# Two state-space mixers: a chunk of 128 tokens is worked as two blocks of 64 on the halves of the partitions

## The chip, the cores and the metric

The kernel runs on one core of one Trainium2 chip, in one launch. The metric is the device time of that launch in microseconds (us). An engine's name in the profile: PE is the tensor engine (matmuls), PEld its weight loads, DVE the vector engine, ACT the scalar engine, POOL the GpSimd engine, SP the engine that issues most DMAs. SBUF is the on-chip memory of 128 partitions, PSUM the matmuls' output memory, eight banks of 512 fp32 values on each of 128 partitions.

## The reference, cut to what matters

Four layers follow each other on x of 4 sequences x 1024 tokens x 512 channels, fp32, each as `x = x + layer(layernorm(x))`: mixer A, a feed-forward layer, mixer B, the same feed-forward layer again. The two mixers are state-space layers. After an input projection, a causal convolution of four taps and silu, both compute, for every head with channels p,

```
state[t] = state[t-1] * exp(a[t]) + (dt[t] * x[t]) outer B[t]      a[t] = -exp(A_log) * softplus(...)
y[t]     = C[t] . state[t] + D * x[t]
```

Mixer A has 16 heads of 64 channels and a state of 64 values for each channel, mixer B 64 heads of 16 channels and a state of 128. Reference A writes the recurrence in chunks of 64 tokens: inside a chunk `M = (C B^T) * exp(segment sums of a)` and `Y_diag = M x`, between chunks a carried state, `Y_off = exp(cumsum a) * (C . state)`. Reference B is a scan over tokens with the same result. The kernel may choose its own chunks.

## The kernel before, in words

Tokens go in chunks of P = 128, two chunks (GC) to a group of 256 tokens; a sequence has 8 chunks, four sequences 32 chunks, 16 groups. A mixer runs over its groups. For each group `front` projects (`convolve`, `gate`: fp32 matmuls of 128x128 weights on 256 or 259 columns, L347), and for each chunk `chunk` does the recurrence. The engines PE, DVE, ACT and POOL run exactly in the order in which the program writes their instructions. `chunk` is a generator: at each `yield us` it lets the driving loop at the end of `mixer` put in pieces of the next group's `front` (a gate counts 1.75, a convolution 1.9) until the yielded amount is used up. `small` and `later_on` hold short steps (transposes, `project_dt`, sums) that are slipped in behind single large matmuls.

What `chunk` does, with the names and lines that matter later:

- `decays(t)`: for 16 heads, the decay matrices exp(cs[l] - cs[s]) for all 128 x 128 pairs of tokens. Four PSUM banks `seg`, four heads in each: first a mask for the pairs in the wrong order inside each half (L797, bf16, two matmuls of 64x64 with 256 columns per bank, -32768 where masked), then the difference of sums as a product of 21 rows with 512 columns (L807, fp16, the four row groups of the array; row 20 masks the upper right quarter), then exp on ACT into `L` (L814, 128x512 at a time).
- `weigh`: DVE multiplies `L` by `Gm` = C B^T with the triangle (L821, 128x1024 at a time).
- `inner`: the weighted sums over source tokens, fp32 matmuls of 128 rows (tokens) x 32 channels in mixer B (four tiles beside each other in the array's columns), 128x64 in A (two tiles), 128 columns each (L837), into the one PSUM bank `py`. Mixer B has four sets of 16 heads (`decays(0)` to `decays(3)`), A one.
- `from_state`: C . state (L855) and its scaling on DVE into `yo` (L859); `open_y` transposes `yo` into `py` (L868); `close_y` adds `py` to h (L886), squares on ACT, multiplies by the gate on POOL (L890).
- the state: POOL makes `hdr` (L927) and scales the old state (L936); `to_state` multiplies (L906) and DVE adds (L917).
- `tail` is the output projection of the chunk before (L669) and its norm; it stands behind the first `decays` of a chunk. `lay_sums`, at the chunk's end, issues on SP the DMAs that bring the cumulated sums of the next chunk from DRAM into the rows `past` and `upto`.

Every fp32 matmul of the program is two MATMUL records in the profile, one for each of two passes. PSUM: seven banks `mm`, handed round, and one for `py`. In mixer B `left`, the last 12 of the 32 tiles, also get the last steps of the first feed-forward layer inside `norm`, which adds DVE work there.

Of the kernel before, what the change touches and what calls it, by code (L numbers as in the profile page):

```python
# [9 lines left out]
BF16 = mybir.dt.bfloat16  # L10
# [5 lines left out]
P = 128  # L16
GC = 2
GT = GC * P
D = 512
# [7 lines left out]

A_MIN = -200.0  # L30
# [42 lines left out]
def hybrid_kernel(  # L73
# [85 lines left out]
    )  # L159

    later = const.tile([P, P], BF16, tag="later", name="later")
    nc.vector.tensor_scalar(later, le, 1.0, -MASKED, ALU.subtract, ALU.mult)
    ident16 = const.tile([P, P], BF16, tag="ident16", name="ident16")
    nc.vector.tensor_copy(ident16, ident)
# [18 lines left out]
    flags = const.tile([P, 2 * HB + 3], F32, tag="flags", name="flags")  # L183
    heads4, first2, row20 = flags[:, :HB], flags[:, 2 * HB : 2 * HB + 1], flags[:, 2 * HB + 2 :]
    pasts = [const.tile([P, SETS, P], F16, tag=f"past{i}", name=f"past_{i}") for i in range(2)]
    sums = [const.tile([P, SETS, HB, P], F16, tag=f"upto{i}", name=f"upto_{i}") for i in range(2)]

    def lay_constants():
        eye = ident.rearrange("p (r w) -> p r w", w=32)
        for i, at in enumerate(  # L190
            [slice(2 + h + 10 * lo, 7 + h + 10 * lo, 4) for lo in (0, 1) for h in range(HB)]
            + [slice(10 * lo, 10 * lo + 2) for lo in (0, 1)]
            + [slice(20, 21)]
        ):
            nc.vector.tensor_reduce(flags[:, i : i + 1], eye[:, :, at], mybir.AxisListType.XY, ALU.add)
        nc.vector.scalar_tensor_tensor(
            heads4, flags[:, HB : 2 * HB], 1.0 / LO_SCALE, heads4, ALU.mult, ALU.add
        )
        nc.vector.scalar_tensor_tensor(
            first2, flags[:, 2 * HB + 1 : 2 * HB + 2], 1.0 / LO_SCALE, first2, ALU.mult, ALU.add  # L200
        )
        for past in pasts:
            nc.vector.tensor_scalar_mul(
                past.rearrange("p t s -> p (t s)"), first2.to_broadcast([P, SETS * P]), -1.0
            )
            nc.vector.tensor_scalar(past[:, :, 64:], past[:, :, 64:], row20, None, ALU.add)

    def lay_flags(sets):
        for upto in sums:
            for t in sets:  # L210
                nc.vector.tensor_copy(upto[:, t], heads4.unsqueeze(2).to_broadcast([P, HB, P]))
                nc.vector.scalar_tensor_tensor(
                    upto[:, t, :, :64],
                    row20.unsqueeze(1).to_broadcast([P, HB, 64]),
                    MASKED,
                    upto[:, t, :, :64],
                    ALU.mult,
                    ALU.add,
                )
# [27 lines left out]
    def mixer(m, in_w, conv_w, conv_b, dt_bias, A_log, Dv, norm_w, out_w, src, dst, first, stats, last_steps={}):  # L247
# [9 lines left out]
        LB = 4  # L257
        SH = P // N
        SW = E // SH
        NE = 2 * NH + NH // SH  # L260
# [5 lines left out]
        with stack:  # L266
            wk = stack.enter_context(tc.tile_pool(name=f"wk_{m.name}", bufs=1, reuse_waits="tile"))
            sm = stack.enter_context(tc.tile_pool(name=f"sm_{m.name}", bufs=2, reuse_waits="tile"))
            p_mm = stack.enter_context(tc.tile_pool(name=f"mm_{m.name}", bufs=7, space=PSUM))
# [119 lines left out]
            def norm(f, prev):  # L389
# [35 lines left out]
                xnT = f.xnT = wk.tile([P, KD, HIST + GT], F32, tag="xnT", name=f"xnT_{tag}", bufs=3)  # L425
# [17 lines left out]
            def front(f, behind):  # L443
# [34 lines left out]
                def silu(j):  # L478
# [13 lines left out]
                    if j % 2 == 0:  # L492
                        f.hs.append(wk.tile([P, 2, GT], F32, tag="h", name=f"h_{tag}_{j}", bufs=8))
                    nc.vector.scalar_tensor_tensor(f.hs[-1][:, j % 2, :], th, 1.0, u, ALU.add, ALU.mult)
# [24 lines left out]
                def gate(n):  # L519
# [14 lines left out]
                    if q == 1:  # L534
                        tz = wk.tile([P, 512], F32, tag="t2k", name=f"tz_{tag}_{rr}", bufs=4)
# [8 lines left out]
                def softplus():  # L544
# [6 lines left out]
                    exu = wk.tile([P, 512], F32, tag="t2k", name=f"exu_{tag}", bufs=4)  # L551
# [21 lines left out]
                    parts = wk.tile([P, 512], F32, tag="t2k", name=f"parts_{tag}", bufs=4)  # L573
# [19 lines left out]
                    ncs = wk.tile([P, 512], F32, tag="t2k", name=f"ncs_{tag}", bufs=4)  # L593
# [63 lines left out]
            state = {"S": None, "tail": iter(())}  # L657

            def tail(f, c, sqs):
# [7 lines left out]
                for e in range(KE):  # L667
                    on = dict(start=(e == 0), stop=(e == KE - 1))
                    nc.tensor.matmul(pout, f.hs[e // 2][:, e % 2, cols], w_out[:, e, :], **on)  # L669
                po = wk.tile([P, D], F32, tag="t2k", name=f"out_{tag}", bufs=4)  # L670
# [34 lines left out]
            def prologue(f, c):  # L705
# [7 lines left out]
                def turn(half, q):  # L713
# [3 lines left out]
                    nc.tensor.transpose(tp[:, q * P : (q + 1) * P], f.hs[half * 2 + q // 2][:, q % 2, cols], ident)  # L717
# [13 lines left out]
                def skip(half):  # L731

                    for e in range(4 * half, 4 * half + 4):
                        h = f.hs[e // 2][:, e % 2, cols]
                        nc.scalar.activation(h, h, AF.Identity, scale=Dc[:, e : e + 1])

                def sums_of(q):
# [5 lines left out]
                    elif q < 3:  # L743
                        nc.tensor.matmul(
                            misc[:, P + (q - 1) * NH : P + q * NH], (le, gt)[q - 1], f.a[:, c, :], start=True, stop=True
                        )
                    elif q == 3:
                        for i in range(SH):
                            nc.tensor.matmul(
                                misc[i * N : i * N + N, P + 2 * NH : P + NE],  # L750
                                ones[:, :N],
                                f.a[:, c, i * NH // SH : (i + 1) * NH // SH],
                                start=True,
                                stop=True,
                                skip_group_check=True,
                            )
                    else:
                        nc.tensor.transpose(misc[:, P + NE : P + NE + N], f.Bc[:, cols], ident[:N, :N])
                        Gm = wk.tile([P, P], F32, tag="Gm", name=f"Gm_{tag}", bufs=2)
                        nc.vector.tensor_mul(Gm, misc[:, :P], le)  # L760
# [10 lines left out]
            def chunk(f, c, following):  # L771
# [13 lines left out]
                el, er, et = ea[:, :NH], ea[:, NH : 2 * NH], ea[:, 2 * NH :]  # L785
# [4 lines left out]
                def decays(t):  # L790

                    sg = [mm(f"seg_{tag}_{t}_{r}").rearrange("p (h l) -> p h l", h=HB) for r in range(4)]

                    for r in range(4):
                        for q in range(2):
                            at = slice(64 * q, 64 * q + 64)
                            nc.tensor.matmul(  # L797
                                sg[r][at, :, at],
                                ident16[at, at],
                                later[at, at].unsqueeze(1).to_broadcast([64, HB, 64]),  # L800
# [4 lines left out]
                    for r in range(4):  # L805
                        rows = slice(32 * r, 32 * r + 21)
                        nc.tensor.matmul(  # L807
                            sg[r], past[rows, t, :], upto[rows, t], start=False, stop=True, skip_group_check=True
                        )
                    Ls = []  # L810
                    for r0 in (0, 2):
                        L = wk.tile([P, 2, HB, P], F32, tag="L", name=f"L_{tag}_{t}_{r0}", bufs=LB)
# [5 lines left out]
                def weigh(Ls):  # L818
                    for L in Ls:
                        Lr = L.rearrange("p r h l -> p (r h) l")  # L820
                        nc.vector.tensor_mul(Lr, Lr, Gm.unsqueeze(1).to_broadcast([P, 2 * HB, P]))  # L821
# [4 lines left out]
                def inner(t, Ls, half, py, started):  # L826

                    for n in range(2 * HB):
                        if CG == 4:

                            u, cg = divmod(n, CG)
                            e, r, hq = 2 * t + half, cg // 2, cg % 2 * 2 + u
                        else:
                            r, hq = divmod(n, HB)
                            e, cg, u = 4 * half + 2 * r + hq // 2, hq % 2, 0
                        h = e * HT + cg * HC + u
                        nc.tensor.matmul(  # L837
                            py[cg * CT : (cg + 1) * CT, e % 4, :],
                            hdt[:, h // HC, u : u + HC, :],
                            Ls[half][:, r, hq, :],  # L840
                            start=not started[cg],
                            stop=False,
                            skip_group_check=True,
                        )
                        started[cg] = True
# [3 lines left out]
                def from_state():  # L849

                    pos = []
                    for half in range(2):
                        rows, hsl = state_at(half)
                        po = mm(f"po_{tag}_{half}")
                        nc.tensor.matmul(po, Cc[rows, cols], state["S"][rows, hsl], start=True, stop=True)  # L855
                        pos.append(po)
                    for half, po in enumerate(pos):
                        tmp = wk.tile([P, 512], F32, tag="yo", name=f"yo_{tag}_{half}", bufs=2)
                        nc.vector.tensor_mul(  # L859
                            heads_of(tmp), heads_of(po), over_head(el[:, half * HALF : (half + 1) * HALF], P, HALF)  # L860
# [3 lines left out]
                def open_y(half):  # L864
                    py = p_y.tile([P, 4, P], F32, tag="y", name=f"py_{tag}_{half}")
                    if not begin:
                        for q in range(4):
                            nc.tensor.matmul(  # L868
                                py[:, q, :],
                                tmps[half][:, q * P : (q + 1) * P],  # L870
                                ident,
                                start=(q == 0),
                                stop=False,
                                is_transpose=True,
                                skip_group_check=True,
                            )
                    return py, [not begin] * CG
# [3 lines left out]
                def close_y(half, py):  # L881

                    sq = wk.tile([P, 4, P], F32, tag="sq", name=f"sq_{tag}_{half}", bufs=2)
# [596 lines left out]
```

## Time and profile before

| | |
|---|---|
| time, median of 3 runs (lowest, highest) | 3009.26 us (3006.67, 3010.05) |
| span of the profiled execution, first to last instruction | 3010.1 us, 46168 instructions |
| mixer A, 75 to 1050 us of the span | PE busy 958.53 of 975 us, DVE 683.30, ACT 386.56, POOL 211.16 |
| mixer B, 1360 to 2765 us | PE busy 1271.17 of 1405 us, DVE 1051.88, ACT 627.50, POOL 298.90 |
| matmul records | 17156 |

The page gives no time of the profiled execution other than its span; the three runs lie within 3.4 us of it. Busy time of PE is the union of records whose ends are modelled: a record lasts some 0.16 us longer than it holds the array, so in dense work start-to-start distances tell the cost and durations don't. In the timeline a row is a run of like instructions: start, length to the last end, count; in brackets the idle time before it and what ended it. "DVE L_b L821" means that the wait ended with the instruction of line 821 that writes a tile named L of mixer B.

### The profile page before, as it was taken

The page shows a single profiled execution, that of the slowest core. Times are in us where ns is not written, and L with a number is a line of the kernel's source. Part 1 is how long each engine was busy: PE and PEld are TensorE (multiplying, and loading weights), DVE is VectorE, ACT ScalarE, POOL GpSimd, SP SyncE. Part 2 cuts the span into 40 slices and gives each one's busy share as a digit, 9 for nine tenths or more (in the row PEclk, how much of TensorE's full clock was granted, in tenths as well). Part 3 has the DMA queues.
Part 4 walks back from the last instruction along what each step waited for, and adds up shares of the span by engine and source line. Part 5 has one row for each costly group of instructions (what it writes and reads, how often), then busy time and mean ns, then how long its engine had stood idle before and what let it go on. Part 6 is the DMA issues. An engine that isn't in the chain of part 4 may idle for free. (4 is left out here: it accounts for less than half of the span.)

```text
span 3010.1 us, 46168 instructions
## 1 busy us (share of the span) xinstructions
PE 2761.4 (92%) x17156; PEld 1785.4 (59%) x17156; DVE 2085.2 (69%) x4417; ACT 1259.9 (42%) x2874; POOL 721.1 (24%) x839
## 2 busy tenths in 40 slices
PE   7999999999999989989999999998989889898986
PEld 6666666666666643456666656666656566564332
DVE  5677677666777652677777677767788777876268
ACT  3334434443344332454444444444444444444244
POOL 1122122222222220531211111212232222212057
PEclk9999999999999989999999999999999999999998
DMA  3000000000000025520000000000000000002423
GB/s 119 10 24 17 17 17 24 18 17 17 21 20 17 10 94 188 177 76 15 11 19 21 20 14 20 15 13 24 20 24 24 18 24 20 13 12 83 160 95 105
DMA packets 92960, 124.27 MB, mean 41 GB/s; under 512 B 38728, under 2 KB 42328, under 8 KB 92736
## 3 DMA queue, kind: packets, MB, share of 16 engines
q1 hardware_dynamic: 80960, 98.23, 10.2%
q10 hardware_dynamic: 9792, 16.82, 1.5%
q0 software_dynamic: 1984, 6.26, 0.6%
q8 instruction: 137, 2.24, 0.3%
q14 instruction: 87, 0.71, 0.1%
HBM read 84.54 MB, written 36.72 MB: 40 GB/s over the span
## 5 line engine op out<-in xcount | busy, mean ns | idle before, releaser
L347 PE MATMUL pc_b<-xnT_b,w_in_b 128*128 128x259 f32 x1280 | 358.0, 408 | 17.8 <-DVE S_b L917 16.7
L821 DVE TENSOR_TENSOR L_b<-L_b,Gm_b 128x1024 f32<-128x1024 f32 x256 | 308.9, 1249 | 2.8 <-ACT L_b L814 2.8
L347 PE MATMUL pz_a<-xnT_a,w_in_a 128*128 128x256 f32 x1024 | 303.5, 410 | 3.0 <-ACT Bt_a L764 2.3
L347 PE MATMUL pc_a<-xnT_a,w_in_a 128*128 128x259 f32 x1152 | 302.5, 397 | 0.0
L347 PE MATMUL pz_b<-xnT_b,w_in_b 128*128 128x256 f32 x1024 | 298.7, 402 | 3.2 <-ACT xnT_b L436 3.2
L814 ACT ACTIVATE L_b<-seg_b 128x512 f32<-128x512 f32 x512 | 263.4, 600 | 78.2 <-PE seg_b L807 78.1
L474 DVE SCALAR_TENSOR_TENSOR u_b<-pc_b,cw_b,u_b 128x256 f32<-128x256 f32 x480 | 231.7, 483 | 84.5 <-ACT u_b L470 73.0
L347 PEld LDWEIGHTS pc_b<-xnT_b,w_in_b 128*128 128x128 f32 x1280 | 229.4, 199 | 84.5 <-DVE S_b L917 20.3
L837 PE MATMUL py_b<-L_b,hdt_b 128*32 128x128 f32 x4096 | 162.8, 294 | 109.3 <-DVE L_b L821 108.3
L474 DVE SCALAR_TENSOR_TENSOR u_a<-pc_a,cw_a,u_a 128x256 f32<-128x256 f32 x432 | 208.5, 483 | 78.5 <-ACT u_a L470 68.2
L1218 PE MATMUL g_ps<-gw,xnT_f 128*128 128x512 f32 x512 | 251.7, 629 | 11.3 <-DMA gw<-in_L_ffn_gate_w 4.6
L347 PEld LDWEIGHTS pc_a<-xnT_a,w_in_a 128*128 128x128 f32 x1152 | 202.8, 192 | 59.5 <-DVE rs_a L684 11.4
L669 PE MATMUL pout_a<-w_out_a,h_a 128*128 128x512 f32 x512 | 230.3, 603 | 0.0
L669 PE MATMUL pout_b<-w_out_b,h_b 128*128 128x512 f32 x512 | 228.3, 599 | 0.0
L890 POOL TENSOR_TENSOR h_b<-h_b,z_b 128x256 f32<-128x256 f32 x128 | 91.3, 734 | 508.7 <-ACT sq_b L889 508.7
L347 PEld LDWEIGHTS pz_b<-xnT_b,w_in_b 128*128 128x128 f32 x1024 | 175.7, 196 | 48.8 <-issue 28.0
L837 PEld LDWEIGHTS py_b<-L_b,hdt_b 128*32 128x32 f32 x4096 | 110.3, 115 | 158.6 <-DVE L_b L821 63.8
L347 PEld LDWEIGHTS pz_a<-xnT_a,w_in_a 128*128 128x128 f32 x1024 | 169.1, 194 | 48.8 <-ACT out_a L689 19.7
L1218 PEld LDWEIGHTS g_ps<-gw,xnT_f 128*128 128x128 f32 x512 | 95.1, 199 | 126.9 <-issue 117.0
L669 PEld LDWEIGHTS pout_a<-w_out_a,h_a 128*128 128x128 f32 x512 | 95.5, 192 | 116.0 <-issue 111.9
L669 PEld LDWEIGHTS pout_b<-w_out_b,h_b 128*128 128x128 f32 x512 | 94.6, 190 | 114.6 <-issue 111.3
L889 ACT ACTIVATE sq_b<-h_b 128x256 f32<-128x256 f32 x128 | 47.9, 417 | 260.5 <-DVE h_b L886 260.5
(321 smaller groups left out, 4903.9 us busy)
## 6 DMA issues: line engine op xcount, KB each, us to landing
d<-in_L_ffn_d_w SPq DMA_DIRECT2D x4, 2048.0 KB
x_f<-xa SPq DMA_DIRECT2D x32, 256.0 KB
xb<-x_b ACTq DMA_DIRECT2D x32, 256.0 KB
x_f<-xb SPq DMA_DIRECT2D x32, 256.0 KB
x_a<-in_L_attn_a_x SPq DMA_DIRECT2D x30, 256.0 KB
xa<-x_a ACTq DMA_DIRECT2D x30, 256.0 KB
out<-x_f SPq DMA_DIRECT2D x22, 256.0 KB
xf<-x_f SPq DMA_DIRECT2D x20, 256.0 KB
```

Of the source, the lines that this page charges most:

```text
L347: nc.tensor.matmul(*args, **kw)
L474: nc.vector.scalar_tensor_tensor(u, ps[:, k : k + GT], cw[:, j, k : k + 1], u, ALU.mult, ALU.add)
L669: nc.tensor.matmul(pout, f.hs[e // 2][:, e % 2, cols], w_out[:, e, :], **on)
L814: nc.scalar.activation(L[:, r], sg[r0 + r], AF.Exp)
L821: nc.vector.tensor_mul(Lr, Lr, Gm.unsqueeze(1).to_broadcast([P, 2 * HB, P]))
L837: nc.tensor.matmul(py[cg * CT : (cg + 1) * CT, e % 4, :], hdt[:, h // HC, u : u + HC, :], Ls[half][:, r, hq, :], start=not started[cg], st ...
L889: nc.scalar.activation(sr, yh, AF.Square)
L890: nc.gpsimd.tensor_mul(yh, yh, zs[half * 2 + r][:, :, cols])
L1218: nc.tensor.matmul(ps, xnT[:, k, :], gw[:, k, :], start=(k == 0), stop=(k == KD - 1 and not bias_on_pe))
```

## The change

A chunk is still 128 tokens, but is treated as two blocks of 64 (BL, NQ = 2), one on partitions 0 to 63, one on 64 to 127.

- Decays are made inside the blocks only: `L` has 64 columns per head in place of 128. One call of `decays` fills its four banks with two sets of 16 heads in mixer B (NS = 2; in A NS = 1 and half a bank each), so B has two calls in place of four and half as many exps and weighs.
- The masks become products too: 24 constant rows (`mask_past`, `mask_upto`, fp16), one 24x64 weight tile and 512 columns (256 in A) per bank and block, and 7 further constant rows inside `past` and `upto` (27 rows in place of 21). The weight tiles are 32 rows x 64 columns of the array, eight of them.
- `inner` becomes matmuls of 64 rows (tokens) x 32 channels (64 in A) with 64 columns, one for each block, into two PSUM banks `py[0]`, `py[1]`.
- Between the blocks the state is carried: POOL scales the old state S0 into `S1`, `to_state` adds the first block's product to it, POOL scales that into `S2`, and the second block's product is added to it behind `weigh(L0)`. `from_state` uses S0 for the first block and S1 for the second, so the first chunk of a sequence now has a `from_state` (second block) and the last a `to_state` (first block). `hdr` is kept in the buffer of S2. The state's products move to the front of the chunk, before `weigh(L0)` and `from_state`.
- Banks: `mm` 6 in place of 7, `py` 2 in place of 1. `xnT` 2 buffers in place of 3; the tiles `h` hold four channel tiles in place of two; `yo` moves into the pool `t2k` (5 buffers in place of 4). The amounts yielded are others. A is cut at -88 in place of -200.

The core of the diff:

```diff
                 def decays(sets):
+                    for r in range(4):
+                        rows = slice(32 * r, 32 * r + 24)
+                        for b, at in enumerate(blocks):
+                            nc.tensor.matmul(sg[r][at].rearrange("p t h l -> p (t h) l"), mask_past[rows, b, :],
+                                mask_upto[rows].unsqueeze(1).to_broadcast([24, NS * HB, BL]), start=True, stop=False, ...)
-                            nc.tensor.matmul(sg[r][at, :, at], ident16[at, at], later[at, at]...to_broadcast([64, HB, 64]), ...)
-                        rows = slice(32 * r, 32 * r + 21)
-                        nc.tensor.matmul(sg[r], past[rows, t, :], upto[rows, t], start=False, stop=True, ...)
+                    for n, t in enumerate(sets):
+                        for r in range(4):
+                            rows = slice(32 * r, 32 * r + 27)
+                            for at in blocks:
+                                nc.tensor.matmul(sg[r][at, n], past[rows, t, at], upto[rows, t, :, at], ...)
-                        L = wk.tile([P, 2, HB, P], F32, tag="L", ..., bufs=LB)
+                        L = wk.tile([P, 2, NS, HB, BL], F32, tag="L", ..., bufs=LB)
                             nc.scalar.activation(L[:, r], sg[r0 + r], AF.Exp)
...
                 def inner(t, Ls, half, py, started):
+                    for n in range(2 * HB // CG):
+                        for b, at in enumerate(blocks):
+                            for cg in range(CG):
+                                nc.tensor.matmul(py[b][cg * CT : (cg + 1) * CT, e % 4, :],
+                                    hdt[at, h // HC, u : u + HC, :], Ls[half][at, r, t % NS, hq, :], ...)
-                        nc.tensor.matmul(py[cg * CT : (cg + 1) * CT, e % 4, :], hdt[:, h // HC, u : u + HC, :], Ls[half][:, r, hq, :], ...)
...
                 def to_state(part):
+                    pst = [mm(f"pst_{tag}_{part}_{b}") for b in range(1 if end else NQ)]
+                            nc.tensor.matmul(pst[b][rows], Bt[blocks[b]], hdr[blocks[b], half * 512 : half * 512 + 512], ...)
+                        nc.vector.tensor_add(S1[:, hsl], S1[:, hsl], pst[0])          # a copy at the sequence's start
+                    if not end:
+                        nc.gpsimd.tensor_mul(heads_of(S2[:, hsl]), heads_of(S1[:, hsl]), over_head(over, P, 512 // HD))
+                    return hsl, pst[-1]
...
-                L0 = decays(0)
+                L0 = decays(range(NS))
                 next(last, None)
-                if not begin:
-                    from_state()
+                nc.gpsimd.tensor_mul(hdr...)
+                if not begin:
+                    nc.gpsimd.tensor_mul(heads_of(S1), heads_of(S0[:, :SW]), over_head(et[0], P, NH // SH))
+                yield 2.2
+                carried = [to_state(part) for part in range(2 // SH)]
+                weigh(L0)
+                if not end:
+                    for hsl, pst in carried:
+                        nc.vector.tensor_add(S2[:, hsl], S2[:, hsl], pst)
+                next(last, None)
+                yield 2.8
+                from_state()
                 if CG == 4:
+                    L1 = decays(range(NS, TS))
+                    yield 2.8
+                    py, on = open_y(0)
+                    for t in range(NS):
+                        for half in range(2):
+                            inner(t, L0, half, py, on)
+                    weigh(L1)
+                    yield 2.4
+                    close_y(0, py)
+                    yield 2.4
+                    py, on = open_y(1)
+                    for t in range(NS, TS):
+                        for half in range(2):
+                            inner(t, L1, half, py, on)
+                    yield 2.0
+                    close_y(1, py)
```

`open_y` now has for each half and each of the four channel tiles two transposes of 64 rows x 128, one per block; `close_y` adds the two banks, 256 values each; the sums of `a` over a block (`misc`) take two matmuls in place of one. New constants are laid once at the start of the kernel, on POOL and DVE.

## The prediction

> **What bounds the kernel now.** I read the page's busy shares first, then the busy time by stage, then PE's waits in each mixer, then the timeline of a chunk.
>
> ```profile
> PE 2761.4 (92%) x17156; PEld 1785.4 (59%) x17156; DVE 2085.2 (69%) x4417; ACT 1259.9 (42%) x2874; POOL 721.1 (24%) x839
> ```
>
> ```profile
> 75.00:1050.00 975.00, 958.53 (x5177) 647.88 (x5178) 683.30 (x1604) 386.56 (x969) 211.16 (x277) 1.00 0.06 17
> ...
> 1360.00:2765.00 1405.00, 1271.17 (x9731) 862.10 (x9729) 1051.88 (x2010) 627.50 (x1456) 298.90 (x316) 0.96 0.07 21
> ```
>
> The rows by stage give length, then PE, PEld, DVE, ACT, POOL, granted clock. Mixer A (first) is PE: 16 us idle in 975, clock 1.00. Mixer B is PE with holes: 134 us idle in 1405, clock 0.96. These two stages hold all that changes. PE's waits in B:
>
> ```profile
> PE py_b L837 <- DVE L_b L821: 108.3, 86, 5.3
> PE pc_b L347 <- DVE S_b L917: 16.7, 12, 2.2
> ```
>
> So `inner` of B waits for DVE's weighing, up to 5.3 us at a time. The pieces of a chunk that the change rewrites, in B and then in A:
>
> ```profile
> 1964.74 0.60 PE L868 MATMUL py_b<-ident,yo_b 128*128 128x128 f32 x4
> 1965.27 1.08 PE L837 MATMUL py_b<-L_b,hdt_b 128*32 128x128 f32 x32
> 1966.28 2.00 PE L347 MATMUL pz_b<-xnT_b,w_in_b 128*128 128x256 f32 x8
> ...
> 1973.51 1.04 PE L717 MATMUL tph_b<-ident,h_b 128*128 128x128 f32 x8
> ...
> 1982.81 1.88 PE L855 MATMUL po_b<-S_b,Cc_b 128*128 128x512 f32 x4
> 1984.53 0.60 PE L347 MATMUL pz_b<-xnT_b,w_in_b 128*128 128x256 f32 x2
> ...
> 1989.81 0.62 PE L797 MATMUL seg_b<-later,ident 64*64 64x256 bf16 x8
> 1990.36 0.39 PE L807 MATMUL seg_b<-upto,past 21*128 21x512 f16 x4
> 1990.69 0.61 PE L678 MATMUL ssq_b<-ones,sq_b 128*128 128x1 f32 x4
> ...
> 2000.61 1.98 PE L906 MATMUL pst_b<-hdr_b,Bt_b 128*128 128x512 f32 x4
> 2002.42 0.60 PE L347 MATMUL pz_b<-xnT_b,w_in_b 128*128 128x256 f32 x2
> ```
>
> ```profile
> 510.76 1.13 PE L855 MATMUL po_a<-S_a,Cc_a 64*128 64x512 f32 x4
> 511.82 0.70 PE L347 MATMUL pz_a<-xnT_a,w_in_a 128*128 128x256 f32 x2
> ...
> 522.69 1.09 PE L837 MATMUL py_a<-L_a,hdt_a 128*64 128x128 f32 x16
> 523.71 3.77 PE L347 MATMUL pc_a<-xnT_a,w_in_a 128*128 128x259 f32 x16
> ```
>
> From start to next start: a `decays` costs 1990.69 - 1989.81 = 0.88 us, a burst of 32 `inner` records in B 1.01, one of 16 in A 1.02, `po_b` 1.72, `pst_b` 1.81, `po_a` 1.06. Eight full transposes last 1.04 with the last record 0.27 long: 0.77 / 7 = 0.11 us per 128 fp32 columns. Thus B's 32 records are eight rounds of four tiles at 0.11 (0.88) and 0.13 for entering and leaving the tiled mode. Tiles in different columns run beside each other; so do different rows: the four products of L807 (385 ns each by its group) are over in 0.39, and two row tiles at a time do `po_a`'s four 512-column records in 1.06, where `po_b` in full width takes 1.72.
>
> **The change part by part, on PE.** I take a round of 64 columns as half of 0.11, 0.055.
> 1. `decays`. Before 128 calls in B, 32 in A: 113 and 28 us. L807's 512-column stream with leaving the mode is 0.33, so 0.22 of it stream. After, in B: masks one round of eight tiles with 512 columns (0.22), products two rounds with 256 (0.22), mode 0.11: 0.55, 64 calls, 35 us; in A half the columns, 0.33 x 32 = 11. Gain 78 + 17. If only four tiles go at once: 1.0 x 64 and 0.55 x 32, gain 49 + 10.
> 2. `inner`. Before 128 bursts in B x 1.01 = 129, 64 in A x 1.02 = 65: 194 us for 5120 records. After 10240 records with half the columns: in B 64 bursts of 128, eight tiles at once, 16 rounds x 0.055 + 0.15 = 1.03, 66 us; in A 64 bursts of 32, four at once, 8 x 0.055 + 0.15 = 0.59, 38 us. Gain 90. Nothing in the trace shows rows and columns of fp32 tiles together. The other end is half as many tiles at once, at the old 0.11 per round: 64 x 3.65 + 64 x 1.9 = 355, a loss of 160. I take the gain, since rows alone and columns alone both run beside each other; with half the tiles and 0.055 it is 1.9 and 1.03 per burst, 188, a gain of 6.
> 3. `open_y`: eight transposes of 64 rows in four pairs, each loading 128 columns of weights as before: same stream, one more mode change per half (0.1 x 128 halves), +13; ends -26 (a pair at 0.055) and +53 (no pairs).
> 4. State products: same streams, in pairs. B newly enters tiled modes, 0.1 x 3 x 32 = +10. First and last chunks of the four sequences gain work: B (1.72 + 0.3 + 1.81) x 4 = 15, A (1.06 + 0.3 + 1.0) x 4 = 9. Together +34; ends +20 and +60.
> 5. One more sum matmul per block in `misc`: +7. The new constants at the start stand on DVE and POOL before the first convolution: some 16 short operations of 0.2 to 0.5 us, +5 (0 to 10).
> PE's work: -78 - 17 - 90 + 13 + 34 + 12 = -126 us.
>
> One rule speaks against part 2. The Trainium skill, "TensorE: Matmul & The Clock Gate", "Back-to-back issue gap", puts a floor of about 25 ns under each matmul of up to 64 columns. By it 10240 records would need 256 us against 194, and the total below would come out near 2959. The row of L807 disagrees for different tiles: its four records of 385 ns are over in 0.39 us, so that their starts lie within some 10 ns.
>
> **The waits.** DVE in B loses half of L821:
>
> ```profile
> L821 DVE TENSOR_TENSOR L_b<-L_b,Gm_b 128x1024 f32<-128x1024 f32 x256 | 308.9, 1249 | 2.8 <-ACT L_b L814 2.8
> ...
> L814 ACT ACTIVATE L_b<-seg_b 128x512 f32<-128x512 f32 x512 | 263.4, 600 | 78.2 <-PE seg_b L807 78.1
> ```
>
> that is -154 us on DVE and -132 on ACT, both beside PE. It gains 120 - 56 = 64 state additions of 0.68 (+44) and contention: L980 needs 425 ns at best and up to 2042 with a POOL operation running, and now POOL's S2 product runs beside `weigh(L0)`; 1 us per chunk, +32 (0 to 60). DVE comes to about 975 us. POOL gains one state product per chunk (about 2 us), off the path: it has the 7 us of `tail` for `hdr` and S1. SP's DMAs keep their place.
>
> The 108 us go: L0 is weighed two pieces and a `from_state` before `inner` reads it. Late next is the scaled state `yo`. Between `pst` and `yo` DVE must do S1 (1.4), two weighs with contention (3.5), S2 (1.4), the tail's row of short operations (2.6), two convolutions with silu (3.7), `yo` (1.4): 14 us. (The tail's row waits for POOL's rsqrt, which now stands behind S2 in POOL's queue; S2's 2 us are over while DVE weighs.) PE in the meantime has `pst` 1.8, two to three pieces with their small matmuls at about 2.2, `po` 1.7, `decays` 0.55: 8.5 to 10.7. It is the same queue that holds the banks: four of six `mm` banks stay with `pst`, two of them until S2. I price the new waits at 2.6 us in each of B's 32 chunks, 83 us against the 134 idle now: -51; ends -134 (nothing waits) and +25 (5 us per chunk). The clock of 0.96 costs 4% of 1405 = 56 us; shorter waits should bring half back, -28; ends 0 and -56. In A one bank less and one more addition: 0 to +30, I take +2.
> Sum: 3010.1 - 126 - 51 - 28 + 2 = 2807 us; the profiled execution stands 0.8 us above the median of the runs, which I leave.
>
> **Rivals.**
> - Narrow tiles give nothing (`inner` 188 us in place of 104): 2807 + 84 = 2891. For it: no row shows eight fp32 tiles. Against: both halves of the claim are shown alone.
> - The waits only move (idle time and clock stay): 2807 + 79 = 2886, with 5 us per chunk 2965. For it: DVE at 975 of some 1220 us is busier than now, 80% against 75%. Against: the longest waits, 5.3 us, have their cause removed.
> - Slower, by one mechanism: the pace of records in `inner`. Today's 5120 records cost 38 ns each with their loads. If the 10240 need 35 ns (rounds not wider than today and not shorter), the loss of 160 replaces the gain of 90: 3057. It decides from 30 ns per record, (104 + 203) / 10240.
> - All waits vanish and the clock returns to 1.00: 2807 - 83 - 28 = 2696.
>
> **How the numbers follow.** About 0.2%, 6 us, is what a measurement can tell from no change. Chances: forecast 0.58 (its own range 2735 to 2860), narrow tiles give nothing 0.14, waits only move 0.13, slower 0.10, all waits vanish 0.05. The range 2720 to 2970 leaves out the last, the slower one and the tail of the third. Faster: 0.58 + 0.14 + 0.05 + 0.11 = 0.88, of which I keep 0.87; same 0.02; slower 0.11.
>
> **What will show it.** Step 1: `decays` start to next start near 0.55 us, exps of B 256 in place of 512. Step 2: 128 records of `inner` in about 1.0 us; at 1.9 the first rival, at 3.6 the slower one. Step 3: eight transposes in 0.55. Waits: L821 gone from PE's waits, L859 or L917's successors in their place, B's idle time near 80 us and its clock near 0.98. The prediction is wrong if PE's waits in B exceed today's 134 us, or A, now without slack, gets longer.

## The result and the profile after

The changed kernel takes 3257.28 us (median of 4 runs, 3247.85 to 3266.32) against 3007.97 us beside it (4 runs): ratio 1.0824, 95% interval 1.0805 to 1.0843. It is some 250 us slower, where 200 us faster was forecast. Its profiled execution spans 3264.6 us, 254.5 us more than that of before.

I cut both executions at the first and the last `pout` record of each mixer. The rows by stage (length, then PE, PEld, DVE, ACT, POOL busy, granted clock, DMA share and rate), A and then B, before:

```profile
100.20:1120.70 1020.50, 995.56 (x5370) 667.84 (x5367) 707.02 (x1655) 400.58 (x1005) 222.81 (x291) 0.99 0.07 22
...
1400.70:2777.70 1377.00, 1246.06 (x9513) 841.38 (x9510) 1029.85 (x1963) 609.09 (x1410) 294.31 (x311) 0.96 0.07 22
```

and after:

```profile
106.20:1268.80 1162.60, 1037.20 (x7085) 688.89 (x7086) 733.50 (x1717) 370.41 (x995) 270.56 (x323) 0.94 0.06 20
...
1550.30:3031.60 1481.30, 1256.02 (x14022) 836.39 (x14023) 995.34 (x1941) 486.11 (x1161) 398.62 (x374) 0.90 0.07 20
```

A is 142 us longer, B 104; the rest of the program accounts for 8. PE's idle time (length minus busy) goes from 24.9 to 125.4 us in A and from 130.9 to 225.3 in B: 195 of the 254 us. Busy time rises by 42 and 10 us although there is less to do, while the granted clock falls from 0.99 to 0.94 and from 0.96 to 0.90. DVE's busy time changes by +26 and -35 us, ACT's falls in both. So the time is lost in waiting and in the slower matmuls after it. PE's waits after (us in total, times, longest):

```profile
PE seg_a L854 <- DVE u_a L516: 69.0, 15, 4.9
PE seg_b L854 <- DVE u_b L516: 68.5, 42, 3.4
PE py_a L945 <- DVE yo_a L933: 48.4, 31, 6.1
PE py_b L945 <- DVE h_b L963: 40.7, 16, 5.0
...
PE pout_b L715 <- DVE u_b L516: 28.1, 6, 4.7
PE seg_b L854 <- DVE hdt_b L767: 23.3, 16, 3.1
...
PE py_b L945 <- DVE yo_b L933: 4.0, 1, 4.0
```

The wait of before, `inner` for weighing, is gone, as forecast. The wait that the forecast put a price on, `open_y` of B for `yo`, occurs once (the last row). PE waits elsewhere, above all at the masks (`seg`, the first matmuls of `decays`), for convolutions (`u`, L516) whose results they don't read: what they need is a PSUM bank that a convolution still holds. The same place in mixer A, before (PE, then ACT):

```profile
497.36 5.53 PE L347 MATMUL pc_a<-xnT_a,w_in_a 128*128 128x259 f32 x24
502.82 0.62 PE L797 MATMUL seg_a<-later,ident 64*64 64x256 bf16 x8
503.37 0.40 PE L807 MATMUL seg_a<-upto,past 21*128 21x512 f16 x4
503.70 7.13 PE L669 MATMUL pout_a<-w_out_a,h_a 128*128 128x512 f32 x16
...
503.58 1.52 ACT L419 ACTIVATE xn_a<-x_a,mv_a 128x512 f32<-128x512 f32 x2 [2.69 <-DVE mv_a L417]
```

and after (PE, then ACT in the wait):

```profile
487.61 0.31 PE L854 MATMUL seg_a<-mask_upto,mask_past 24*64 24x256 f16 x6
492.79 0.29 PE L854 MATMUL seg_a<-mask_upto,mask_past 24*64 24x256 f16 x2 [4.88 <-DVE u_a L516]
493.01 0.83 PE L866 MATMUL seg_a<-upto,past 27*64 27x256 f16 x8
493.99 10.01 PE L715 MATMUL pout_a<-w_out_a,h_a 128*128 128x512 f32 x16 [0.15 <-ACT L_a L878]
...
488.60 1.52 ACT L461 ACTIVATE xn_a<-x_a,mv_a 128x512 f32<-128x512 f32 x2 [3.67 <-DVE mv_a L459]
490.02 0.70 ACT L972 ACTIVATE sq_a<-h_a 128x256 f32<-128x256 f32 x2
490.64 0.54 ACT L512 ACTIVATE u_a<-pc_a,cb_a,cw_a 128x256 f32<-128x256 f32 x1
```

Six masks fill three banks; the fourth comes 4.88 us later. ACT cannot read the waiting convolution (L512) before the norm of a later group (L461), which waits for DVE. The banks are handed out in turn. After, three convolutions, a gate and the masks go round six of them, and the fourth mask comes to the bank of the second convolution, which is not read yet. Before, ACT had a wait of the same kind here (2.69 us), but PE did not have to wait: three convolutions (the 24 records) and four masks came out at exactly seven banks, and `pout` took the bank of the first convolution, which had been read. And the 16 records of `pout` behind the wait take 10.01 us instead of 7.13. The granted clock in these stretches (seventh figure) says why:

```profile
487.60:492.70 5.10, 0.32 (x7) 0.12 (x6) 2.73 (x9) 3.46 (x8) 1.09 (x2) 1.00 0.00 0
492.70:496.00 3.30, 3.06 (x13) 1.67 (x14) 3.07 (x11) 1.63 (x5) 0.00 (x0) 0.55 0.00 0
496.00:500.00 4.00, 4.00 (x7) 1.54 (x6) 2.83 (x12) 0.00 (x0) 0.00 (x0) 0.52 0.00 0
500.00:503.00 3.00, 3.00 (x9) 1.33 (x8) 0.00 (x0) 0.00 (x0) 0.00 (x0) 1.00 0.00 0
```

For 7 us after the wait the array runs at half clock: records of 512 columns start every 853 ns, not 429. Over the whole execution, stretches in which `pout`, the projections and the gate of the feed-forward layer start at twice their usual distance add up to some 240 us, before to some 55; half of that is lost.

### The profile page after: what moved, and what is told of

Same layout as the page of the kernel before. It is cut to its first block, busy times and chain, and to the rows that moved or that the text cites. A ratio compares the mean times of both kernels' runs of the same rounds, so it can differ in the third digit from the quotient of the medians.

```text
span 3264.6 us, 59019 instructions
## 1 busy us (share of the span) xinstructions
PE 2813.0 (86%) x23620; PEld 1801.3 (55%) x23620; DVE 2086.2 (64%) x4507; ACT 1106.1 (34%) x2618; POOL 879.5 (27%) x954
## 5 line engine op out<-in xcount | busy, mean ns | idle before, releaser
L389 PE MATMUL pc_b<-xnT_b,w_in_b 128*128 128x259 f32 x1280 | 382.4, 433 | 9.2 <-DVE yo_b L933 8.4
L516 DVE SCALAR_TENSOR_TENSOR u_b<-pc_b,cw_b,u_b 128x256 f32<-128x256 f32 x480 | 231.9, 483 | 193.0 <-ACT u_b L512 181.5
L389 PE MATMUL pc_a<-xnT_a,w_in_a 128*128 128x259 f32 x1152 | 320.8, 413 | 0.0
L715 PE MATMUL pout_b<-w_out_b,h_b 128*128 128x512 f32 x512 | 265.2, 677 | 44.0 <-DVE u_b L516 28.1
L389 PEld LDWEIGHTS pc_b<-xnT_b,w_in_b 128*128 128x128 f32 x1280 | 250.1, 215 | 79.2 <-DVE yo_b L933 18.7
L516 DVE SCALAR_TENSOR_TENSOR u_a<-pc_a,cw_a,u_a 128x256 f32<-128x256 f32 x432 | 208.5, 483 | 98.1 <-ACT u_a L512 87.6
L715 PE MATMUL pout_a<-w_out_a,h_a 128*128 128x512 f32 x512 | 266.3, 680 | 3.3 <-ACT L_a L878 3.2
L885 DVE TENSOR_TENSOR L_b<-L_b,Gm_b 128x1024 f32<-128x1024 f32 x128 | 185.6, 1490 | 0.9 <-ACT L_b L878 0.9
L878 ACT ACTIVATE L_b<-seg_b 128x512 f32<-128x512 f32 x256 | 131.7, 601 | 154.5 <-PE seg_b L866 148.5
L854 PEld LDWEIGHTS <-mask_past 24*64 24x64 f16 x768 | 28.8, 104 | 271.6 <-issue 138.0
L854 PE MATMUL seg_b<-mask_upto,mask_past 24*64 24x512 f16 x512 | 73.5, 425 | 113.3 <-DVE u_b L516 68.5
L969 POOL TENSOR_TENSOR h_a<-h_a,z_a 128x256 f32<-128x256 f32 x128 | 91.0, 731 | 287.9 <-DVE h_a L963 287.9
```

The lines of the kernel that those rows point to most:

```text
L389: nc.tensor.matmul(*args, **kw)
L516: nc.vector.scalar_tensor_tensor(u, ps[:, k : k + GT], cw[:, j, k : k + 1], u, ALU.mult, ALU.add)
L715: nc.tensor.matmul(pout, f.hs[e // 4][:, e % 4, cols], w_out[:, e, :], **on)
L854: nc.tensor.matmul(sg[r][at].rearrange("p t h l -> p (t h) l"), mask_past[rows, b, :], mask_upto[rows].unsqueeze(1).to_broadcast([24, NS * ...
L878: nc.scalar.activation(L[:, r], sg[r0 + r], AF.Exp)
L969: nc.gpsimd.tensor_mul(yh, yh, zs[half * 2 + r][:, :, cols])
```

## The experiments

The theories: (1) the bank that `py[1]` took from `mm` is missing; (2) the state's work, moved to the chunk's front, makes DVE and POOL late, in the order in which they must work; (3) the many narrow matmuls pull the clock down by themselves. All times below are medians of 4 or 5 runs beside 7 or 8 of the kernel before; "A" and "B" are lengths from first to last `pout` of the profiled execution (before 1020.5 and 1377.0, after 1162.6 and 1481.3).

**The kernel before with six banks.**

```diff
-p_mm = ... tc.tile_pool(name=f"mm_{m.name}", bufs=7, space=PSUM)
+p_mm = ... tc.tile_pool(name=f"mm_{m.name}", bufs=6, space=PSUM)
```

> The kernel before with six banks `mm` in place of seven; the eighth bank of PSUM stays unused. Nothing else differs. Theory 1 (the lost bank): PE's new waits stand at the masks of `decays`, which need four banks while three are still held by convolutions that ACT and DVE have not read. Then the kernel before must get the same waits: in mixer A 16 waits of about 4.9 us and the half-clock stretches behind them, 16 x (4.9 + 2.1) = +112 us, in B +60 to +130 us; 3180 to 3250 us. Theory 2 (the state work moved to the front holds DVE and POOL, so that the readers of the banks are late): the old order reads its banks in time, and six are enough: 3005 to 3040 us. Theory 3 (many narrow matmuls lower the clock by themselves): as theory 2, since this kernel has none.

3131.37 us, ratio 1.0388 (1.0373 to 1.0404): +120 us. A 1107.3 (+87), B 1402.6 (+26). Its rows by stage and the longest new wait of A:

```profile
106.40:1213.70 1107.30, 1029.81 (x5366) 683.21 (x5367) 704.07 (x1652) 397.47 (x997) 222.74 (x291) 0.96 0.06 20
1495.00:2897.60 1402.60, 1253.18 (x9514) 841.18 (x9511) 1037.87 (x1965) 612.73 (x1410) 295.42 (x312) 0.97 0.07 21
```

```profile
PE pout_a L669 <- DVE u_a L474: 56.3, 15, 4.7
```

Fifteen waits of up to 4.7 us for a convolution's bank, once per group, and without one of the change's narrow matmuls; half clock follows seven of them. They stand at `pout`, not at the masks as I had expected. In A theory 1 explains 87 of 142 us (expected 112), in B only 26 of 104, where I had expected 60 to 130. The total lies below the 3180 to 3250 us of theory 1 and well above the 3005 to 3040 of the other two.

**Two banks more for A.** Sixteen heads in two row groups with two sets of sums, so that `decays` fills two whole banks in place of four halves.

```diff
-TS = NH // 16
+RG = 4 if NH > 16 else 2
+TS = NH // (4 * RG)
 ...
-sg = [mm(...) for r in range(4)]
+sg = [mm(...) for r in range(RG)]
```

> The changed kernel, but mixer A's decays fill two whole banks (two row groups, two sets of sums each) in place of four half banks, so that A has two banks more to hand round at each chunk's head. Mixer B is untouched. The masks and products of A stream 0.2 us longer per chunk, +7 us. Theory 1 (the lost bank): the 15 waits of 4.9 us at A's masks and the half-clock stretches of `pout` behind them go, -105 + 7: near 3160 us, mixer A near 1065 us from its first to its last `pout`. Theory 2 (DVE and POOL are late whatever the banks): the wait moves to the next matmul that needs a convolution's or a state's result; 3235 to 3265 us. Theory 3 (narrow matmuls lower the clock): the waits go, but `pout` still runs in half clock behind the masks: about 3190 us.

3184.89 us, ratio 1.0570 (1.0552 to 1.0587). A 1080.0, 83 us less (near 1065 expected); B 1493.8, 12 us longer though nothing in it was changed. So the total misses the 3160 us of theory 1. The masks' wait is gone, and `pout` in A, still right behind the narrow matmuls, is back at full pace (227 us from start to next start, after 261, before 228). That refutes theory 3 at this place; against it elsewhere speaks the last run below, which has all the narrow matmuls at a granted clock of 0.99 in A and 0.95 in B, before 0.99 and 0.96. But a part of the wait has moved:

```profile
PE ssq_a L725 <- DVE a_a L613: 38.6, 14, 2.8
```

**`pout` ahead of the first `decays`.**

```diff
-L0 = decays(range(NS))
 next(last, None)
+L0 = decays(range(NS))
```

> The changed kernel with one exchange: the output projection of the chunk before (`pout`, one bank, 7 us) stands ahead of the chunk's first `decays` (four banks) in both mixers, not behind. Theory 1 (the lost bank): in these 7 us ACT and DVE free the convolutions' banks, and the masks find four: A -105 us; in B the waits at the first masks (1.35 us in every second chunk) and at `pout` (44 us) go with half as much of clock behind them, -75; near 3080 us. Theory 2 (DVE and POOL late whatever the banks): the waits move to `pout` or to the state products behind it, 3220 to 3265 us.

3187.70 us, ratio 1.0581 (1.0561 to 1.0601). A 1088.2 (-74), B 1486.7: nothing. In A the order does nearly what two banks did (-105 was expected), with 34.2 us at `ssq` here too. In B the 44 us at `pout` are gone and 57.9 us at `ssq` (for DVE's fold of squares) stand in their place. Theory 2 held for B.

**The second `decays` later in B.**

```diff
 from_state()
 if CG == 4:
-    L1 = decays(range(NS, TS))
     yield 2.8
     py, on = open_y(0)
     ... inner(t, L0, half, py, on)
-    weigh(L1)
+    L1 = decays(range(NS, TS))
     yield 2.4
     close_y(0, py)
+    weigh(L1)
```

> As the run with `pout` first, and in mixer B the second `decays` is moved from its place right behind `from_state` to behind the first `inner`, its weighing behind the first `close_y`. Theory 1 (the lost bank): at the old place four banks of state products and two of `from_state` are still held; the waits at the second masks (15 of 3.4 us, and 15 times 1.2 + 0.8 + 0.3 + 0.6) go, some 94 us and 30 of half clock: 120 us below the run with `pout` first, near 2960 us. Theory 2: no gain, the second weighing comes later and `inner` waits for it: at or above the run with `pout` first.

3134.80 us, ratio 1.0412 (1.0393 to 1.0432). B 1437.3, 49 us less, not 120: the masks' waits for convolutions are gone, but 58.1 us for weighing (L885) came, and 45.0 us (14 waits, up to 6.7) of `open_y` for `yo`: the wait that the prediction had put a price on shows once the masks no longer stand before it.

**Without POOL's scaling of the state,** on the changed kernel.

```diff
-nc.gpsimd.tensor_mul(heads_of(S1), heads_of(S0[:, :SW]), over_head(et[0], ...))
-nc.gpsimd.tensor_mul(heads_of(S2[:, hsl]), heads_of(S1[:, hsl]), over_head(over, ...))
```

> The changed kernel without POOL's two products that scale the carried state (S0 into S1, S1 into S2); left out is thus the decay of the state between blocks, all else is issued as before. Theory 2a (these products hold DVE: its S additions wait for them and its other operations stretch beside them, and that holds the banks): POOL loses about 4 us per chunk of B and 2.6 of A, DVE's waits and stretching shrink by half, PE idles 60 to 100 us less, with the clock 3257 falls to 3120 to 3190 us. Theory 1 (six banks in the order of the change are short whatever POOL does): 3230 to 3260 us.

3157.10 us, ratio 1.0494 (1.0458 to 1.0529): 100 us less, A 1108.5 and B 1426.7, 54 us each. DVE's weighing, after, and without these products (busy, mean ns of one):

```profile
L885 DVE TENSOR_TENSOR L_b<-L_b,Gm_b 128x1024 f32<-128x1024 f32 x128 | 185.6, 1490 | 0.9 <-ACT L_b L878 0.9
L885 DVE TENSOR_TENSOR L_a<-L_a,Gm_a 128x512 f32<-128x512 f32 x64 | 64.9, 1055 | 0.0
```

```profile
L885 DVE TENSOR_TENSOR L_b<-L_b,Gm_b 128x1024 f32<-128x1024 f32 x128 | 150.6, 1218 | 0.9 <-ACT L_b L878 0.9
L885 DVE TENSOR_TENSOR L_a<-L_a,Gm_a 128x512 f32<-128x512 f32 x64 | 41.1, 684 | 0.0
```

POOL's products were called off the path, and the contention that was counted on DVE did not enter the time. They lie on it: what DVE does beside them stretches (684 to 1055 ns). DVE's busy time falls by 36 us in A and 60 in B without them, PE's idle time by 35 and 34. That DVE's state additions wait for POOL, as the expectation had it, does not show in the changed kernel, where those behind POOL's second product have no idle time before them:

```profile
L1016 DVE TENSOR_TENSOR S_b<-S_b,pst_b 128x512 f32<-128x512 f32 x56 | 35.6, 674 | 0.0
```

So stretching is what the profile shows; that banks stay occupied for longer by it, and PE waits for them, is argued.

**The scaled state `yo` ahead of weighing.** On the run with `pout` first and L1 late:

```diff
 carried = [to_state(part) ...]
-weigh(L0)
+yield 1.4
 S2 += pst
-next(last, None)
-yield 2.8
 from_state()
+weigh(L0)
+next(last, None)
-yield 2.8  (A: 2.0)
+yield 4.2  (A: 3.4)
```

> As the run with `pout` first and the second `decays` late (3134.8 us), and `from_state` with its scaling into `yo` stands ahead of `weigh` of the first set and of the tail's row of short operations, behind both state additions. Theory 2b (the scaled state is late because weighing and the tail's row stand ahead of it in DVE's queue): PE's waits of 46 us in A and 45 in B for `yo` go, with a little half clock: 3025 to 3060 us. Rival (the wait for POOL's second state product, now directly ahead of `yo`, takes their place): 3110 to 3150 us.

3142.20 us, ratio 1.0438 (1.0409 to 1.0467): the rival's range, but not by its mechanism, since DVE waits for POOL's second state product only 0.6 us in A and 0.2 in B. The waits for `yo` are gone but for 1.7 us in A, but `open_y` of A now waits 30.5 us for `close_y`, and `pout` of B 37.2 for POOL's gating. A is 20 us longer, B 23 shorter.

**And the sums of squares later.** `tail` hands out `ssq` in a step of its own, called behind the state products.

```diff
-defer(rs, [... add_squares ...], True)
 later_on.append(copy of pout)
 yield
+defer(rs, [... add_squares ...], True)
+yield
```

> As the run with `yo` first, and the sums of squares of the chunk before (`ssq`) are handed out only behind the state products, not behind the first large matmul of the chunk. Theory 2c (PE's waits of 34 us in A and 55 in B at `ssq` come from its place in PE's order, ahead of DVE's fold that stands behind the softplus steps): these waits go, 90 to 120 us below the run with `yo` first. Rival (DVE is late as a whole, and the next matmul that needs it waits instead): within 30 us of it.

3050.50 us, ratio 1.0137 (1.0111 to 1.0163): 92 us less, as theory 2 said, but divided otherwise than it had it: A 1037.7 (-70), B 1399.7 (-15). In the run with `yo` first `ssq` had 33.4 us of waits in A and only 6.9 in B; B's 55 belonged to the run before that. In A PE had stood in front of `ssq` while the fold of squares waited in DVE's queue behind the softplus steps; nothing but a place in PE's order had to change.

**Both, with two banks in A** (the edit above).

> As the run with late sums of squares, and mixer A's `decays` fill two whole banks in place of four halves. Theory 1 (banks): if A still waits for banks, it gains up to 30 us; if `pout` first has already given the banks time to come free, it only pays the 7 us of longer masks and products.

3044.35 us, ratio 1.0115 (1.0084 to 1.0145). A 1037.3, the same: with `pout` first and `ssq` late, A no longer lacks banks.

**The second `decays` between two yields,** and the state products' banks in another order.

```diff
-psts per part: [b0, b1]
+psts: [part0 b0, part1 b0, part0 b1, part1 b1]
-yield 4.2
+yield 2.4
+L1 = decays(range(NS, TS))
+yield 1.8
 ... inner(t, L0, ...)
-L1 = decays(range(NS, TS))
+weigh(L1)
 yield 2.4
 close_y(0, py)
-weigh(L1)
```

> As the run with late sums of squares and two banks in A (3044 us), with two moves in B: the second `decays` stands between two yields ahead of the first `inner` (where the state's banks are free again) and its weighing behind the first `inner`, ahead of `close_y`; and the four banks of the state products are handed out with the first block's two first, so that `from_state`, six banks later, meets banks that the S1 additions have freed and not one that waits for the S2 addition. Theory 2 (order on DVE and of the banks): PE's waits of 56 us for weighing fall below 25 and those of 30 us within `from_state` go: 2980 to 3005 us, below the kernel before. Rival (DVE has no room left in B, what is moved is waited for elsewhere): 3030 to 3050 us.

3078.64 us, ratio 1.0233 (1.0207 to 1.0259): 34 us worse, a miss. The wait for weighing in the run before, and what came for it:

```profile
PE py_b L903 <- DVE L_b L888: 55.8, 58, 1.5
```

```profile
PE seg_b L856 <- ACT Bt_b L816: 55.2, 15, 4.4
```

The earlier masks now meet the bank of `misc` that ACT has not read; the waits within `from_state` stayed at 30 us, so they were not for the banks that I had reordered.

**More pieces at the chunk's end.**

```diff
-yield 2.0
+yield 1.0
 close_y(1, py)
 ...
-yield 2.4
+yield 3.4
```

> As the run with the second `decays` between two yields, and in B the amount of projection pieces behind the last `inner` is cut from 2.0 to 1.0 and that at the chunk's end raised from 2.4 to 3.4 (2.4 and 1.8, 2.4 become 2.2 and 1.8, 2.2). Theory 2: PE's waits of 37 us at `pout` for POOL's gating of h go: 25 to 40 us below the run with the second `decays` between two yields. Rival: `close_y` now waits for `inner` and holds DVE, no gain or a loss of up to 20 us.

3072.23 us, ratio 1.0216 (1.0189 to 1.0243). The 42 us at `pout` for POOL's gating are gone, but the wait of `open_y` for `close_y`'s additions rose from 41.7 to 66.6. That is 6 us less, where 25 to 40 were expected: the rival's case, what is moved is waited for elsewhere.

**The yields shared out anew,** twice, on the run with late sums and two banks. In A the first run moves 1.0 from behind `from_state` to ahead of it, the second has `from_state` ahead of the S2 addition. The yields of B in order, as they were, in the first and in the second run:

```diff
-2.2, 1.4, 4.2, 2.4, 2.4, 2.0, 2.4
+2.2, 1.8, 3.4, 2.4, 3.2, 1.0, 3.0
+2.2, 1.4, 4.2, 2.4, 3.0, 1.0, 2.8
```

> As the run with late sums of squares and two banks in A (3044 us, PE idle 60 us in A and 187 in B), with the amounts of projection pieces shared out otherwise. A: 2.4 in place of 1.4 ahead of `from_state`, 2.4 in place of 3.4 behind. B: 1.8 and 3.4 around `from_state` (before 1.4 and 4.2), 3.2 in place of 2.4 between the second weighing and the second `inner`, 1.0 in place of 2.0 behind it, 3.0 in place of 2.4 at the chunk's end. If order alone is short: in A the waits of 29 us behind `from_state` shrink by half, in B those for the second weighing (56) and at `pout` (37) by 50 together: 2960 to 3000 us. If DVE has no slack left and waits only move: 3030 to 3060 us.

> As the run with late sums of squares and two banks in A; in A the scaling into `yo` stands ahead of the S2 addition; in B only the end of the chunk is changed: 3.0 in place of 2.4 between the second weighing and the second `inner`, 1.0 in place of 2.0 behind it, 2.8 in place of 2.4 at the end. If order alone is short: 2980 to 3015 us, A as before or 10 us less, B 30 us less. If waits only move: 3030 to 3060 us.

2993.45 us, ratio 0.9923 (0.9895 to 0.9951), and 2984.09 us, ratio 0.9896 (0.9873 to 0.9919): both beat the kernel before, by 0.8 and 1.0%, with the arithmetic of the change. A stays at 1038.4 and 1035.3 (its 29 us behind `from_state` did not move: that expectation of the first run failed), B falls by 46 and 55 us, where 30 were expected of the second. In the first, the waits of B for weighing and at `pout` fall from 93 to 53 us, less than the 50 expected. The last run by stage, and one `decays` of B that waits for nothing:

```profile
99.10:1134.40 1035.30, 975.10 (x6979) 648.53 (x6978) 712.99 (x1727) 373.50 (x1005) 262.78 (x325) 0.99 0.07 22
...
1411.50:2749.00 1337.50, 1188.97 (x14047) 789.46 (x14046) 965.77 (x1947) 485.05 (x1166) 397.54 (x377) 0.95 0.07 22
```

```profile
1935.25 0.42 PE L856 MATMUL seg_b<-mask_upto,mask_past 24*64 24x512 f16 x8
1935.49 0.40 PE L868 MATMUL seg_b<-upto,past 27*64 27x256 f16 x16
1935.82 0.70 PE L390 MATMUL pz_b<-xnT_b,w_in_b 128*128 128x256 f32 x2
```

PE's busy time is 20 us (A) and 57 us (B) below that of before, its idle time 35 and 18 us above. So it is B that gains (39.5 us shorter than before); A is still 15 us longer.

## Why the prediction was wrong

The terms of the sum, one by one.

**Work: right in kind, near in size.** A `decays` of B costs 1935.82 - 1935.25 = 0.57 us (forecast 0.55); in A 0.58, forecast 0.33. `inner` in A takes 0.625 us for 32 records (0.59). In B the 128 records take 1.41, not 1.03:

```profile
2110.85 1.48 PE L900 MATMUL py_b<-L_b,hdt_b 64*32 64x64 f32 x128
2112.26 0.92 PE L389 MATMUL pc_b<-xnT_b,w_in_b 128*128 128x259 f32 x3
```

so 64 x 1.41 + 64 x 0.625 = 130 us against 194 before, a gain of 64 where 90 was forecast: eight fp32 tiles run beside each other, though not at the full pace; 1.41 lies between the forecast and the 1.9 of the first rival. `open_y` is 0.39 us per half (before 0.53), better than the +13. Summed from start to next start with idle time taken out, between the first and last `pout` of the best run against before: `decays` -76 us (forecast -95), `inner` -78 (-90), state products +35 (+34); all of PE's work in A and B together is 78 us less busy. The rival of the record pace fell: 11 ns per record in B, 20 in A, not 30. The Trainium skill, "TensorE: Matmul & The Clock Gate", "Back-to-back issue gap", has a floor of about 25 ns for small matmuls; for different tiles of the array this trace goes below it.

**Waits in B, -51: the step that failed first.** PE's idle time there was to fall from 134 us to 83, and rose from 130.9 to 225.3 between the first and last `pout`. I had seen that four of six banks stay with `pst`, but put a price on one wait alone, that of `open_y` for `yo`. It took 4.0 us, once. In its place PE waited 113 us at the masks (by what ended them, 68.5 for convolutions, 23.3 for `hdt`, 11.2 for `two`, and only 2.4 for the S2 addition, the holder that I had named), 44 at `pout`, and 40.7 in `open_y` for the additions of `close_y`; the upper end (+25, 5 us per chunk at one place) was no bound at all. The 14 us that I counted for DVE between `pst` and `yo` were right (14.1 measured), and my own rows then gave a wait of 14 less 8.5 to 10.7, that is 3.3 to 5.5 us per chunk, where I wrote 2.6 without a reason. DVE's work in B fell by 35 us (1029.85 to 995.34), not by the 77 from 1052 to 975: weighing took 185.6 us, not the half of 308.9. But a sum of an engine's work does not say when it is done. The rival "the waits only move" had a slip too: its 2965 with 5 us per chunk does not follow from its terms, 2886 and 26 us more, 2912.

**A, +2 with 0 to +30: the step that cost most.** PE's idle time there rose from 24.9 to 125.4 us: 69.0 at the masks for a convolution's bank, 48.4 in `open_y` for `yo`, the very wait that had been priced for B. One bank less was worth 87 us there by the run with six banks, 83 by the one with two more. The timeline of before shows that A had no bank to spare at a group's end: for about 4 us from 503.70 on two unread convolutions, four masks and `pout` hold all seven. The rest of A's 142 was mostly order: the late `ssq` brought 70 us in the run with `yo` first (these effects overlap); 15 us of it are still there in the best run.

**Clock, -28:** it followed the waits the other way, to 0.90 in B and 0.94 in A. The sentence "wrong if PE's waits in B exceed today's 134 us, or A gets longer" named both failures, without a rival that carried them.

**POOL "off the path":** 100 us by the run without its products. The 32 us of contention were counted as DVE's work, and none of it as time. The causes overlap: their single effects are not to be added, and how B's 104 us divide among banks, POOL and order is not settled; that the whole loss comes back with another order of the same work is. Not tried alone are the other buffers that the change took: `xnT` with 2 in place of 3 (PE's waits that end with it come to some 14 us in the changed kernel), `h` and `yo`; the best run keeps them all.

## What to carry to other kernels

Before a change takes a PSUM bank, list at the densest moment who holds each bank and until when; a bank that looks spare on average may be the one that hides a delay of ACT or DVE, here of up to 5 us. Price a wait by every in-order queue it stands in, and add what the clock costs behind it (here 2.9 us behind a wait of 4.9). When a cheaper set of instructions runs slower, try the order and the amounts of filling work before giving the instructions up: here the same arithmetic moved from 8.2% slower to 1.0% faster.

## What the runs showed that I had not expected

- Half clock after a wait as short as 1.35 us: at 2164 us in the changed kernel PE waits 1.35 us at the masks, and from 2165.5 to 2169 us the granted clock is 0.51. The masks around that wait are sparse work: PE is busy 2.05 of the 3.4 us from 2162.1 on. A wait of 1.23 us at 2109, with PE busy without a break ahead of it and behind it, has no half clock after it (1.00 from 2110 to 2116). After the 4.88 us wait it lasts 7 us. The Trainium skill, "TensorE: Matmul & The Clock Gate", "Part 1: The HAM clock gate", says that full speed returns after at least one busy window of some 3.4 us; the 7 us agree with "at least", while its "idle window" of 3.4 us is longer than the wait that sufficed here.
- Eight fp32 tiles of 64 x 32 at a time: 11 ns per record.
- The reason why `py` takes two banks is not tried here. The Trainium skill, "TensorEngine Tiling (Array Packing)", "Gotcha 1: PSUM Pressure", says that different row tiles cannot use one PSUM bank at the same time; no run here shows it. The change keeps its two blocks in two half-filled banks, and that is the bank that A lacked.
